# Softmax over heads beside an expert stream: expert sums and weighted values held in one PSUM bank, a third adding transfer for every two blocks, and a longer lead of experts

## The chip, the cores and the metric

The kernel runs on one core of a Trainium2 chip. A core has five engines that work beside each other and wait for each other by semaphores: TensorE (matrix products, PE in the profile, its weight loads PEld), VectorE (DVE), ScalarE (ACT), GpSimd (POOL) and SyncE (SP), which here only issues transfers. Transfers from all issuers run on 16 DMA engines. The metric is the device time of one execution in microseconds; smaller is better.

## The reference

The kernel computes a stack of eight residual layers on x of shape (2, 1024, 128). Only the last two matter here. The seventh is attention whose softmax runs over the 16 heads (axis 1 of batch, head, query, key), not over the keys. The sixth and the eighth are sums over eight gated experts.

```python
def _L1_attn_b_ref(x, w_qkv, b_qkv, w_proj, b_proj):
    qkv = (x @ w_qkv + b_qkv).reshape(b, n, 3, N_HEADS, HEAD_DIM)      # 16 heads of 8
    q, k, v = jnp.transpose(qkv, (2, 0, 3, 1, 4))
    dp = jnp.einsum('bhqd,bhkd->bhqk', q, k) * SCALE
    attn = jax.nn.softmax(dp, axis=1)                                   # over heads
    w_avg = jnp.einsum('bhqk,bhkd->bhqd', attn, v)
    return jnp.transpose(w_avg, (0, 2, 1, 3)).reshape(b, n, dim) @ w_proj + b_proj

def _L1_ffn_ref(x, Wg, Wu, Wd):                                         # 8 experts, 128 -> 512 -> 128
    return sum(jax.nn.silu(x @ Wg[e]) * (x @ Wu[e]) @ Wd[e] for e in range(8))

x = x + _L1_ffn_ref(_layernorm(x), ...)
x = x + _L1_attn_b_ref(_layernorm(x), ...)
x = x + _L1_ffn_ref(_layernorm(x), ...)
```

Because the softmax is over heads, a block of 128 queries and 128 keys needs nothing of any other block: for each of its 128x128 positions it takes the maximum over 16 heads, 16 exponentials, their sum and its inverse.

## The kernel before

All activations stay in x_res, 16 tiles of 128 tokens by 128 channels; all of the work below is float32. `first_layer` does the first six layers, up to the experts of chunks 0 and 1. Then `experts_ffn(g, w, [2])` does the experts of chunk 2 of the sixth layer (512 tokens: 32 units, one per expert and quarter of its hidden width), `heads_and_experts(g, w, [6, 7], [0, 1, 2, 3, 4, 5])` does the head softmax with an expert stream beside it, and `experts_ffn(g, w, [3])` the last experts.

**The head loop.** `heads_and_experts` writes out the order of every engine's instructions by hand (`tc.manual_schedule`). It walks 128 blocks: 2 batches, 8 query tiles, 8 key tiles. In its round i it starts block i+1 and carries older ones further. The stages of a block, with lines:

- `products` (L1194): TensorE forms the scores of all 16 heads in the four-bank PSUM tile h_s, 4 matmuls of 512 columns. There is one h_s, so the next scores wait until this block's subtraction has read it.
- `maxima` (L1205) and the subtraction (L1211) on VectorE; the result goes to h_e in SBUF, 4 buffers.
- the exponentials (L1214) on ScalarE in two halves.
- `lower` (L1220): SyncE copies heads 0 to 7 to a tile of half the size; `upper` (L1224): GpSimd issues a transfer that adds heads 8 to 15 to it. Eight sums of two heads stand there.
- `denominators` (L1229): TensorE adds these eight with identity matmuls, 8 of 128 columns, into h_pd.
- `inverse` (L1234): VectorE takes the reciprocal.
- `normalize` (L1239): GpSimd multiplies h_e by it into a second tile h_a.
- `weigh` (L1245): TensorE multiplies with the values in h_vz, 16 matmuls, into h_po. After the eighth key tile ScalarE copies h_po to h_oT (L1340), and the next round projects it (L1309) and adds it to x_res (L1318).

Round i does the scores, maximum, exponentials and `lower` of block i+1, `upper` of block i, the denominators of i-1, inverse and normalising of i-2, weighing of i-3.

**The expert stream.** `ExpertStream` feeds the same units in chunks of 256 tokens. In each round `products` (L1043) takes up to two units, each with a gate and an up product of 256 columns in one bank of e_pgu (two banks), `gates` (L1050) is the Silu on ScalarE, `multiply` (L1058) the product on VectorE, and in the next round `outputs` (L1069) multiplies by Wd, four matmuls of 128 columns, and `add` (L1078) adds them to x_res. Silu and Exp lie in different activation tables, so each round holds two table loads on ScalarE.

**The shared bank.** `outputs`, the projection and `denominators` all write h_pd, for which there is one PSUM bank. So in a round TensorE's outputs wait for the inverse that reads the last denominators, and its denominators wait for the additions that read the outputs.

**Side work.** Opening a chunk (a layer norm, two transposes) and the preparation of a batch (norm, transposes, projections) are lists of steps tagged with an engine. `aside(place)` takes one such step when the round comes to that engine; where TensorE gets a step, the round takes no expert units. Ahead of the loop the steps of batch 0 run with a round of the stream behind each. Behind the loop the stream runs alone until it is empty.

**Norms.** `StagedNorm` has three stages: statistics on VectorE, a square root on ScalarE, an inverse on VectorE. `apply_on_act` forms the shift -mean/deviation with one VectorE instruction (L74) for all tiles and applies it on ScalarE (L76); `apply` does it on GpSimd (L82).

Of the kernel before, what the change touches and what calls it, by code (L numbers as in the profile page):

```python
# [19 lines left out]
P = 128  # L20
# [28 lines left out]
class StagedNorm:  # L49
# [20 lines left out]

    def apply_on_act(self, dst):

        shift = self.g.small.tile([P, self.nt], F32, name=f"{self.key}_nb", bufs=2)
        self.g.nc.vector.scalar_tensor_tensor(shift, self.mv[:, :, 0], -1.0, self.rs, ALU.mult, ALU.mult)  # L74
        for t in range(self.nt):
            self.g.nc.scalar.activation(  # L76
                dst[:, t, :], self.src[:, t, :], AF.Identity, bias=shift[:, t : t + 1], scale=self.rs[:, t : t + 1]
            )
# [746 lines left out]
def linear_steps(g, w, b, seq, bank):  # L825
# [7 lines left out]
    for src, dst in ((xb, u), (u, un)):  # L833
        ln = StagedNorm(g, src, TPB, "l")
        ln.stats(range(TPB))
        ln.root()
        yield
        ln.inverse()
        ln.apply_on_act(dst)
        yield  # L840
# [86 lines left out]
def expert_steps(g, w, chunks, work, ps, ps_o):  # L927
# [6 lines left out]
    def opening(n):  # L934
# [7 lines left out]
        ln.inverse()  # L942
# [58 lines left out]
class ExpertStream:  # L1001

    NE, FC = 8, 4

    def __init__(self, g, w, work, ps):
        self.g, self.w, self.work, self.ps = g, w, work, ps
        self.units, self.fresh, self.gated, self.ready, self.sums = [], [], [], [], []

    def tokens(self, chunk):
        return self.g.x[:, 2 * chunk : 2 * chunk + 2, :]

    def opening(self, chunk):
# [6 lines left out]
        yield "dve", ln.inverse  # L1021
        yield "pool", lambda: ln.apply(u, range(2))

        def transposes():
# [5 lines left out]
            self.units += [(chunk, e, fc, uT) for e in range(self.NE) for fc in range(self.FC)]  # L1030

        yield "pe", transposes

    def products(self):

        nc, w = self.g.nc, self.w
        for _ in range(2):
# [24 lines left out]
    def outputs(self, po):  # L1062

        nc = self.g.nc
        if self.ready:
            two, self.ready = self.ready[:2], self.ready[2:]
            for t in range(2):
                for k, (_, e, fc, h) in enumerate(two):
                    nc.tensor.matmul(  # L1069
                        po[:, t, :], h[:, bass.ts(t, P)], self.w["Wd"][:, e, fc, :], start=(k == 0), stop=(k == 1)  # L1070
                    )
            self.sums.append((two[0][0], po))

    def add(self):

        for chunk, po in self.sums:
            xt = self.tokens(chunk)
            self.g.nc.vector.tensor_add(xt, xt, po[:, 0:2, :])  # L1078
        self.sums = []
# [12 lines left out]
def heads_and_experts(g, w, first, second):  # L1092
# [4 lines left out]
    with ExitStack() as es:  # L1097
# [10 lines left out]

        keep = one.tile([P, K], F32, name="h_keep")
# [12 lines left out]
        ex = ExpertStream(g, w, ework, ps_e)  # L1122
        qzs, kTs, vs = {}, {}, {}

        def preparation(b):

            xb = g.x[:, b * TPB : (b + 1) * TPB, :]
            ln = StagedNorm(g, xb, TPB, "h")
            u = seq.tile([P, TPB, D], F32, name="h_u", bufs=1)
            uT = seq.tile([P, L], F32, name="h_uT", bufs=1)  # L1130
            qzs[b] = seq.tile([P, K, L], F32, name="h_qz")
            kTs[b] = seq.tile([P, L], F32, name="h_kT")
            vs[b] = seq.tile([P, TPB, D], F32, name="h_v", bufs=1)
            for t in range(0, TPB, 2):
                yield "dve", lambda t=t: ln.stats((t, t + 1))
            yield "act", ln.root
            yield "dve", ln.inverse
            for t in range(0, TPB, 2):
                yield "pool", lambda t=t: ln.apply(u, (t, t + 1))


            def bias(t):
                nc.gpsimd.tensor_add(
                    xb[:, t : t + 4, :], xb[:, t : t + 4, :], w["b_proj2"].unsqueeze(1).to_broadcast([P, 4, D])
                )

            def transposes(n):
                pt = ps_e.tile([P, 4, P], F32, name="e_pgu")
                for t in range(4):
# [421 lines left out]
```

## Time and profile before

| | us |
|---|---|
| median of the runs shown | 2253.45 |
| these runs | 2245.86, 2253.45, 2253.84 |
| the profiled execution, own time | 2250.19 |
| its span, first to last instruction | 2248.2 |
| mean granted TensorE clock | 0.945 |

Stages by the profile, in microseconds from the start of the span: up to 1076 the first six layers, to 1165 the experts of chunk 2, to 1228 the preparation of batch 0, from 1227.8 (first scores) to 2122.6 (scores of the last block) the head loop, from 2158.2 the last experts. Busy time in four of these stretches:

| stretch | PE | DVE | ACT | POOL | share of the DMA engines |
|---|---|---|---|---|---|
| 1075 to 1165 | 87.33 of 90 | 23.90 | 23.45 | 1.73 | 0.00 |
| 1165 to 1250 | 66.42 of 85 | 42.90 | 35.28 | 17.19 | 0.10 |
| 1600 to 1760 | 155.18 of 160 | 144.80 | 119.14 | 124.63 | 0.59 |
| 2158 to 2248 | 84.98 of 90 | 22.68 | 21.12 | 0.00 | 0.01 |

A row of the groups view gives line, engine, operation, tiles and shapes, the number of instructions, their busy time, the mean of one in nanoseconds, and then the idle time of the engine just ahead of them with what ended it. A float32 matmul appears as two PE rows (two passes), so 16 rows of L1229 are 8 matmuls. A row of the view in order of time begins with start and duration; x32 behind it says that so many instructions are merged in it. In the transfer view the last number is the median time from the issue of a transfer to its landing.

### The profile page before, as it was taken

Reading aid. Unit: us, or ns where it says so; the run is one execution under the profiler, and the core shown is the slowest. Engines: PE = TensorE matmul, PEld = TensorE weight load, DVE = VectorE, ACT = ScalarE, POOL = GpSimd, SP = SyncE. Lnnn points to the kernel's source line nnn. Section 1 sums busy time; section 2 is a strip of 40 time slices with the busy share of each in tenths; the row PEclk is TensorE's granted clock in tenths of the full one; section 3 lists DMA queues with packets and bytes.
Section 4 is the critical chain, followed back from the end, with each engine's and each line's share of the span. In section 5 each row is a group of like instructions: output and inputs, shape, how many; then the busy total and the mean of one; then the engine's idle time right before and its main releaser. Section 6 shows DMA issues by size and latency. Waiting matters only on the chain. (4 is left out here: it accounts for less than half of the span.)

```text
span 2248.2 us, 36361 instructions
## 1 busy us (share of the span) xinstructions
PE 1967.7 (88%) x14832; PEld 1160.9 (52%) x14832; DVE 1685.6 (75%) x2030; ACT 1215.2 (54%) x1551; POOL 892.7 (40%) x464
## 2 busy tenths in 40 slices
PE   7669888889958758996998898988999999999999
PEld 4323243333334323344445676756777777777753
DVE  5866767898684699874234898988998989998822
ACT  1026512276624667744324675746777777777722
POOL 0013400073401000000001777887777777777710
PEclk9789979989988879998999999999999999999999
DMA  4000000296631386510000555555565555555500
GB/s 89 1 1 1 1 1 1 71 224 155 164 98 49 95 195 163 138 37 1 1 0 5 154 152 151 151 151 151 142 158 147 155 145 148 153 149 151 150 15 5
DMA packets 73799, 220.16 MB, mean 98 GB/s; under 512 B 9184, under 2 KB 19872, under 8 KB 73504
## 3 DMA queue, kind: packets, MB, share of 16 engines
q1 hardware_dynamic: 54736, 149.40, 22.6%
q0 software_dynamic: 18432, 67.12, 15.8%
q8 instruction: 116, 1.90, 0.4%
q10 hardware_dynamic: 464, 1.33, 0.3%
q14 instruction: 51, 0.42, 0.1%
HBM read 78.35 MB, written 5.24 MB: 37 GB/s over the span
## 5 line engine op out<-in xcount | busy, mean ns | idle before, releaser
L1239 POOL TENSOR_TENSOR h_a<-h_e,h_r 128x2048 f32<-128x2048 f32 x128 | 582.9, 4554 | 135.3 <-PE h_po L1245 90.8
L1205 DVE TENSOR_REDUCE h_m<-h_s 128x128 f32<-128x2048 f32 x128 | 293.2, 2291 | 71.1 <-PE h_s L1194 71.0
L1229 PE MATMUL h_pd<-h_e,ident 128*128 128x128 f32 x2048 | 264.4, 283 | 47.1 <-DMA h_e<-h_e 35.3
L1211 DVE TENSOR_TENSOR h_e<-h_s,h_m 128x2048 f32<-128x2048 f32 x128 | 292.4, 2284 | 2.5 <-DVE h_m L1205 0.6
L1214 ACT ACTIVATE h_e<-h_e 128x1024 f32<-128x1024 f32 x256 | 256.5, 1049 | 66.9 <-DVE h_e L1211 62.8
L1229 PEld LDWEIGHTS h_pd<-h_e,ident 128*128 128x128 f32 x2048 | 242.2, 194 | 89.7 <-DVE x_res L1078 46.7
L1050 ACT ACT_TABLE_LOAD x110 | 141.1, 1283 | 172.1 <-PE e_pgu L1043 171.8
L377 POOL TENSOR_SCALAR_AFFINE_SELECT a_pT<-a_pT 128x256 f32<-128x256 f32 x120 | 128.5, 1092 | 204.4 <-ACT a_pT L374 201.6
L279 DVE TENSOR_REDUCE a_nm<-a_s 128x2 f32<-128x1024 f32 (+7 forms) x144 | 168.0, 1217 | 41.2 <-PE a_s L270 27.3
L963 DVE TENSOR_TENSOR e_h<-e_sg,e_pu 128x512 f32<-128x512 f32 x128 | 86.6, 685 | 144.4 <-PE e_pu L956 132.1
L958 ACT ACTIVATE e_sg<-e_pg 128x512 f32<-128x512 f32 x128 | 76.4, 597 | 184.0 <-PE e_pg L955 163.9
L1069 PEld LDWEIGHTS h_pd<-Wd,e_h 128*128 128x128 f32 x1024 | 125.0, 191 | 95.0 <-DVE e_h L1058 78.8
L374 ACT ACTIVATE a_pT<-a_st 128x1024 f32<-128x1024 f32 (+3 forms) x176 | 129.9, 791 | 66.2 <-PE a_st L360 63.6
L1194 PE MATMUL h_s<-h_qz,h_kT 32*128 32x512 f32 x1024 | 148.1, 648 | 16.0 <-DVE h_e L1211 10.8
L792 DVE TENSOR_TENSOR_SCAN s_h<-s_a,s_h 128x1024 f32<-128x1024 f32 x64 | 148.7, 2324 | 17.9 <-ACT s_a L760 14.1
L1224 POOL DMA_DIRECT2D h_e<-h_e x128 | 114.6, 895 | 113.0 <-DMA h_e<-h_e 51.6
L1043 PE MATMUL e_pgu<-e_uT,Wg 128*128 128x256 f32 x512 | 155.0, 385 | 2.6 <-ACT h_qz L1158 2.1
L261 PE MATMUL a_s<-a_latT,a_qT 32*128 32x512 f32 (+3 forms) x768 | 119.8, 599 | 41.8 <-DVE a_nm L279 39.9
L1069 PE MATMUL h_pd<-Wd,e_h 128*128 128x128 f32 x1024 | 149.7, 288 | 6.5 <-DVE e_h L1058 4.7
L956 PE MATMUL e_pu<-e_uT,Wu 128*128 128x512 f32 x256 | 135.5, 612 | 20.4 <-DVE e_h L963 20.4
L1043 PE MATMUL e_pgu<-e_uT,Wu 128*128 128x256 f32 x512 | 152.8, 380 | 0.0
L1214 ACT ACT_TABLE_LOAD x111 | 142.4, 1283 | 13.3 <-issue 6.5
(283 smaller groups left out, 3231.4 us busy)
## 6 DMA issues: line engine op xcount, KB each, us to landing
h_e<-h_e SPq DMA_DIRECT2D x128, 512.0 KB, 4.1
h_e<-h_e POOLq DMA_DIRECT2D x128, 512.0 KB, 4.6
s_a<-s_steps SPq DMA_DIRECT2D x64, 512.0 KB, 5.0
s_h<-s_steps SPq DMA_DIRECT2D x64, 512.0 KB, 6.6
s_steps<-s_gate SPq DMA_DIRECT2D x8, 256.0 KB, 2.1
Wg<-in_Wg_dram SPq DMA_DIRECT2D x8, 256.0 KB, 6.0
Wu<-in_Wu_dram SPq DMA_DIRECT2D x8, 256.0 KB, 5.9
Wd<-in_Wd_dram SPq DMA_DIRECT2D x8, 256.0 KB, 6.1
```

The lines of the kernel that those rows point to most:

```text
L279: nc.vector.tensor_reduce(nm[:, half, i, h : h + together], s[:, :, :n], AX.X, ALU.max, negate=True)
L792: nc.vector.tensor_tensor_scan(h, a, h, 0.0, ALU.mult, ALU.add)
L956: nc.tensor.matmul(pu, w["Wu"][:, e, f], opened[n], start=True, stop=True)
L1043: nc.tensor.matmul(pgu[:, k, :], w[name][:, e, f], uT, start=True, stop=True)
L1050: nc.scalar.activation(sg, pgu[:, 0, :], AF.Silu)
L1069: nc.tensor.matmul(po[:, t, :], h[:, bass.ts(t, P)], self.w["Wd"][:, e, fc, :], start=(k == 0), stop=(k == 1))
L1194: nc.tensor.matmul(s[:, j, :].rearrange("p (k q) -> p k q", k=K), kTs[b][quad, bass.ts(kb, P)], qzs[b][quad, :, bass.ts(qb, P)], start=Tru ...
L1205: nc.vector.tensor_reduce(m, heads.rearrange("p h q -> p q h"), AX.X, ALU.max)
L1211: nc.vector.tensor_sub(e, heads, m.unsqueeze(1).to_broadcast([P, H, P]))
L1214: nc.scalar.activation(eh, eh, AF.Exp, scale=scale)
L1229: nc.tensor.matmul(pd, g.ident, e2[:, k, :], start=(k == 0), stop=(k == 7))
L1239: nc.gpsimd.tensor_mul(a, e, r.unsqueeze(1).to_broadcast([P, H, P]))
```

## The change

Part by part, in the order in which the stages run:

- `experts_ffn(g, w, [2])` goes; the stream's first list becomes chunks 4 to 7, that is, the two half chunks of chunk 2 come into the stream. Ahead of the head loop the stream now runs until at most 76 units are left.
- `preparation` is done in halves of a batch (512 tokens), the query tiles split with it.
- All layer norms of this stage are applied on ScalarE (`apply_on_act`), and the shift is made by `inverse_and_shift` with one VectorE instruction per tile that has one tensor and two per-partition scalars in it. This also replaces the form with two tensors in the other users of `apply_on_act`.
- One PSUM bank, `held`, takes three sums over a longer time: `sums` (256 columns, the output of a whole chunk of the stream), `po` (the weighted values) and `proj` (the projection). ScalarE zeroes a part once it is read out, and all matmuls add. `outputs` becomes one matmul of 256 columns per unit with Wd as the weights; it runs in every second round, on up to four units. The chunk's sum is copied, turned back by two transposes (`turn`) and added to x_res once per chunk.
- h_e2 becomes a tile for a pair of blocks. In even rounds GpSimd issues a third adding transfer, `fours`: for both blocks of the pair it adds the last four sums of two heads to the first four. In odd rounds `denominators` adds four sums of four heads for both blocks, 4 matmuls of 256 columns. The inverse stays one per block.
- `normalize` works in place in h_e, which has 7 buffers now. Every later stage is further behind: denominators of blocks i-3 and i-2 in odd round i, inverse and normalising of i-4, weighing of i-5, projection two rounds after the copy.
- In a round `products` of the stream now stands before `outputs`, and a round with a TensorE side step or a `turn` still takes one unit.
- Some weights move to the pool of the first layers.

```diff
+    def inverse_and_shift(self):
+        self.inverse()
+        self.shift = self.g.small.tile([P, self.nt], F32, name=f"{self.key}_nb", bufs=2)
+        for t in range(self.nt):
+            self.g.nc.vector.tensor_scalar(
+                self.shift[:, t : t + 1], self.mv[:, t, 0:1], self.rs[:, t : t + 1], -1.0, ALU.mult, ALU.mult
+            )
...
-    def outputs(self, po):
+    def outputs(self):
...
+        units, self.ready = self.ready, []
+        for chunk, e, fc, h in units:
+            last = e == self.NE - 1 and fc == self.FC - 1
+            nc.tensor.matmul(
+                self.sums, self.w["Wd"][:, e, fc, :], h, start=False, stop=last, skip_group_check=True
+            )
+            if last:
+                oT = self.work.tile([P, 2 * P], F32, name="e_oT", bufs=1)
+                nc.scalar.copy(oT, self.sums)
+                nc.scalar.copy(self.sums, self.zero.to_broadcast([P, 2 * P]))
+                self.summed.append((chunk, oT))
+    def turn(self):
+        nc = self.g.nc
+        if self.done:
+            chunk, oT = self.done.pop(0)
+            pt = self.ps.tile([P, 4, P], F32, name="e_pgu")
+            for t in range(2):
+                nc.tensor.transpose(pt[:, t, :], oT[:, bass.ts(t, P)], self.g.ident)
+            self.turned = chunk, pt
+            return True
+        self.done, self.summed = self.summed, []
+        return False
...
+        held = ps_o.tile([P, 4 * P], F32, name="h_po")
+        sums, po, proj = held[:, 0 : 2 * P], held[:, 2 * P : 3 * P], held[:, 3 * P :]
...
-            e = work.tile([P, H, P], F32, name="h_e", bufs=4)
+            e = work.tile([P, H, P], F32, name="h_e", bufs=7)
...
+        def fours(pair):
+            nc.gpsimd.dma_start(out=pair[:, :, 0:4, :], in_=pair[:, :, 4:8, :], accum_op=ALU.add)
+        def denominators(pair):
+            pd = ps_d.tile([P, 2, P], F32, name="h_pd")
+            for k in range(4):
+                nc.tensor.matmul(pd, g.ident, pair[:, :, k, :], start=(k == 0), stop=(k == 3))
             return pd
...
         def normalize(e, r):
-            a = work.tile([P, H, P], F32, name="h_a")
-            nc.gpsimd.tensor_mul(a, e, r.unsqueeze(1).to_broadcast([P, H, P]))
-            return a
+            nc.gpsimd.tensor_mul(e, e, r.unsqueeze(1).to_broadcast([P, H, P]))
...
+        def alone():
+            for place in ("dve", "act", "pool", "pe"):
+                aside(place)
+            ex.outputs()
+            ex.turn()
+            ex.add()
+            ex.products()
+            ex.gates()
+            ex.multiply()
...
+            while len(ex.units) + 32 * ex.unopened > 76:
+                alone()
...
+            for i in range(-1, n + 7):
+                now, resting, oT = resting, oT, None
                 if i + 1 < n:
                     heads = products(*blocks[i + 1])
+                even = i % 2 == 0
+                if 0 <= i - 4 < n:
+                    r = inverse(d_[i - 4 - i % 2][:, i % 2, :])
...
+                made, ex.ready = ex.ready, []
                 ex.multiply()
+                fresh, ex.ready = ex.ready, made
+                ex.products(1 if ex.turn() or aside("pe") else 2)
+                if even:
+                    ex.outputs()
+                ex.ready += fresh
...
+                    if not even:
+                        pairs[i + 1] = work.tile([P, 2, 8, P], F32, name="h_e2")
+                    lower(pairs[i + 1 - even][:, int(even)], e_[i + 1])
                 aside("dve")
+                if 0 <= i - 4 < n:
+                    normalize(e_[i - 4], r)
+                if even and 0 <= i - 2 < n:
+                    fours(pairs[i - 2])
                 if 0 <= i < n:
+                    upper(pairs[i - i % 2][:, i % 2], e_[i])
                 aside("pool")
+                if 0 <= i - 5 < n:
+                    b, qb, kb = blocks[i - 5]
+                    weigh(kb, e_.pop(i - 5))
                     if kb == TPB - 1:
...
+                        nc.scalar.copy(held[:, 2 * P :], zero.to_broadcast([P, 2 * P]))
...
+                if not even and 0 <= i - 3 < n:
+                    d_[i - 3] = denominators(pairs.pop(i - 3))
+            while ex.busy() or side or current:
+                alone()
...
-    experts_ffn(g, w, [2])
-    heads_and_experts(g, w, [6, 7], [0, 1, 2, 3, 4, 5])
+    heads_and_experts(g, w, [4, 5, 6, 7], [0, 1, 2, 3, 4, 5])
     experts_ffn(g, w, [3])
```

## The prediction

> **What bounds the kernel now.** I read the page's busy list first, then the stretch views, then one round of the head loop in order of time, then the transfers and the chain that ended last.
>
> ```profile
> span 2248.2 us, 36361 instructions
> ...
> PE 1967.7 (88%) x14832; PEld 1160.9 (52%) x14832; DVE 1685.6 (75%) x2030; ACT 1215.2 (54%) x1551; POOL 892.7 (40%) x464
> ...
> DVE  5866767898684699874234898988998989998822
> ...
> PEclk9789979989988879998999999999999999999999
> ```
>
> TensorE is busiest, but these are shares of the whole span. The tile view of h_s puts the first scores at 1227.8 us and those of the last block at 2122.6 us: 894.8 us for 127 steps, **7.05 us a block**, 40% of the span. Ahead of it stand the experts of chunk 2 (1076 to 1165 us, TensorE busy 87.33 of the 90.00 us in the stretch view) and the preparation of batch 0 (1165 to 1228); behind it lie 35.6 us until the first L955 product of the last experts (2158.2 us). Nothing else is changed in substance. One round, start, duration and engine first, idle time before it in brackets:
>
> ```profile
> 1710.33 1.08 PE L1245 MATMUL h_po<-h_a,h_vz 128*32 128x128 f32 x32
> ...
> 1711.34 1.14 PE L1194 MATMUL h_s<-h_qz,h_kT 32*128 32x512 f32 x8
> 1711.59 4.52 POOL L1239 TENSOR_TENSOR h_a<-h_e,h_r 128x2048 f32<-128x2048 f32 x1 [1.38 <-PE h_po L1245]
> ...
> 1712.41 1.16 PE L1069 MATMUL h_pd<-Wd,e_h 128*128 128x128 f32 x8
> 1712.55 2.29 DVE L1205 TENSOR_REDUCE h_m<-h_s 128x128 f32<-128x2048 f32 x1 [0.55 <-PE h_s L1194]
> ...
> 1713.41 0.60 PE L1043 MATMUL e_pgu<-e_uT,Wg 128*128 128x256 f32 x2
> ...
> 1715.09 2.28 DVE L1211 TENSOR_TENSOR h_e<-h_s,h_m 128x2048 f32<-128x2048 f32 x1
> ...
> 1715.22 2.05 PE L1229 MATMUL h_pd<-h_e,ident 128*128 128x128 f32 x16
> ...
> 1716.07 0.86 POOL L1224 DMA_DIRECT2D h_e<-h_e  x1
> ...
> 1717.20 1.08 PE L1245 MATMUL h_po<-h_a,h_vz 128*32 128x128 f32 x32
> 1717.31 0.96 DVE L1234 RECIPROCAL h_r<-h_pd 128x128 f32<-128x128 f32 x1
> ...
> 1718.19 0.69 DVE L1058 TENSOR_TENSOR e_h<-e_sg,e_pgu 128x256 f32<-128x256 f32 x2
> ```
>
> The reader is to see three chains of the same length. TensorE goes L1245, L1194, L1069, L1043, L1229 with start-to-start 1.01, 1.07, 0.89, 1.92, 1.98: 6.87 us without a real gap. VectorE goes maximum 2.21, addition 0.33 (1714.76 to 1715.09), subtraction 2.22, inverse 0.88, two products 0.66, and waits 0.55 for the next scores. GpSimd works 4.52 + 0.86 and idles. So TensorE sets the round and VectorE is 0.6 us behind. The transfers of the loop (queue, packets, MB, share of 16 engines; then KB and us to landing):
>
> ```profile
> q0 software_dynamic: 18142, 66.06, 39.3%
> q1 hardware_dynamic: 19169, 66.47, 18.8%
> ...
> h_e<-h_e POOLq DMA_DIRECT2D x126, 512.0 KB, 4.6
> h_e<-h_e SPq DMA_DIRECT2D x125, 512.0 KB, 4.2
> ```
>
> Over that stretch of 890 us, 39.3% for 126 adding transfers is 2.78 us of all 16 engines each, and 18.8% for 125 plain ones 1.34 us.
>
> **What the change takes from the loop.** Denominators: two blocks now cost TensorE 4 matmuls of 256 columns, 8 passes, in place of 2x16 passes. L1043 streams 8 such passes in 1.73 us (chain of waits), so a pair costs 1.73 + 0.15 against 2x1.98: 1.04 us off a block. Expert outputs (L1069) become one 256-column matmul a unit: 0.86 against 0.89, nothing; but their VectorE addition goes (0.33 a block), and so does the shared bank in which outputs, addition, denominators and inverse waited for each other. TensorE then needs about 1.01 + 1.07 + 1.92 + 0.86 + 0.94 = 5.80, VectorE 2.21 + 2.22 + 0.88 + 0.66 = 5.97. In-place normalising frees h_a: nothing, L1239 keeps its 4.52.
>
> **What it adds.** GpSimd issues a third transfer per pair. 256 pieces of 2 KB (two runs in each of 128 partitions) stand where the row L1224 has 128 of 4 KB (144 packets each, 16 of them tiny) for 0.88 us, so its price lies between 0.88 and 1.76. [...] I take 1.2. GpSimd: 2x4.52 + 2x0.88 + 1.2 + 0.4 of gaps = 12.4 a pair, 6.2 a block. Transfers: 2x1.34 + 2x2.78 + 2.8 = 11.0 a pair, 5.5 a block. **By resources alone the block would be 6.2 us.**
>
> **The wait that is added.** The third transfer stands on GpSimd's queue behind an even block's normalising, waits for the odd block's adding transfer, and has the second addition and the next normalising queued behind it. Its landing releases the denominators, the last TensorE work of the odd round, with the next scores queued behind them; then come the inverse and the normalising that precedes the next third transfer. That is a ring, one lap a pair:
> - normalising 4.52, and 0.05 to the issue;
> - issue to landing: c;
> - landing to denominators 0.13 (below: 1730.60 + 6.07 to 1736.81 is 0.14);
> - denominators to inverse 1.93 (8 passes of L1043 are busy from 1706.54 to 1708.43, 1.89, and 0.04 as between L1229 and L1234);
> - inverse to normalising 1.15 (L1234 at 1703.35, L1239 at 1704.50).
>
> Sum 7.78 + c. Without c TensorE would reach these denominators about 10.1 us after the inverse (the next inverse 5.97 later by VectorE's row, 1.2 for it and the first product, products 1.9, weighing 1.0), while the transfer is issued 5.7 after it, so only c up to about 4.3 is hidden.
>
> ```profile
> 1730.60 6.07 DMA h_e<-h_e
> 1736.81 2.02 PE h_pd L1229 x16
> ```
>
> c is the whole question. The nearest row is the adding transfer: median 4.6, least 4.5, most 7.1 (line view of L1224); the two lines above show 6.07 and TensorE starting right behind. [...] The row is of an accumulate of the same bytes on the same queue, so the row decides. On the 4.6 I put 0.3 for the longer issue and 0.7 for the plain transfer of the next block. That one now starts later: the changed build makes the exponential's table load (1.28 us, L1214) wait for the subtraction, whereas now the load ends just before it. [...] c = 5.6: lap 13.4, **6.7 us a block**. Ends: 4.6 (6.2 a block, GpSimd decides) and 7.1 (7.44).
>
> Loop: 127 x (6.7 - 7.05) = **-44 us**.
>
> **Around the loop.** Chunk 2's work, 64 units of 256 columns, moves from their own stage into the stream. Built order: 52 units run ahead of the first scores, 232 between first and last scores, 36 behind (before: 32, 214, 10). A lone round of two units takes 3.59 now (additions at 1188.43, 1192.02, 1195.61). The first unit's output no longer waits for the second's product, 0.43 less: 3.16. 26 rounds are 82 us, 5 for the first opening, 13 for six norms with their table loads and the projections (16 rounds now exceed 16x3.59 by 5 with one norm): the loop starts at about 1176 in place of 1228, **-50** rounded. Behind the last scores: five rounds that still carry the ring at 6.4 (32), three short ones (10), ten lone rounds (32), the last sums and opening (8): 82 against 35.6, **+46**.
> Shift from one tensor: seven more VectorE instructions of about 0.1 in each of four norms of the linear attention, the later ones beside ScalarE's 0.40 a tile: **+2**. Norms applied on ScalarE instead of GpSimd (16 e_u and 16 h_u rows, 28 us): ScalarE is busy 5.2 of 6.7, hidden; uncovered, one opening is 0.8. Weights in the early pool and the zeroing copies: nothing, beside the loop.
>
> Sum: -44 - 50 + 46 + 2 = -46 on the profiled run's own 2250.2 us, the span plus 2.0: 2204. The median of the runs, 2253.45, lies 3 us higher, so **2205 us**.
>
> **Rivals.**
> - Resources decide, c near 4.6: 6.2 a block, 127 x -0.85 = -108, total -110: **2140**. For it: the median of 4.6 holds for most adding transfers of the trace. Against: a plain transfer falls into the third one's window. Chance 0.2.
> - The ring closes later than today's round: 256 pieces cost 1.76 to issue, and the whole plain transfer (1.34) goes in between: c = 4.6 + 0.9 + 1.34 + 0.3 = 7.1, lap 14.9, 7.44 a block, +50 - 2: **2298**, slower. It decides from c = 6.35, where 127 x (P - 7.05) passes +2. For it: landings of 5.9 to 6.4 all along the chain that ended last. Chance 0.19.
> - The gain is given back exactly: c about 6.2, P 7.0 to 7.1, **2250**. Chance 0.11.
> - The change doesn't do what it says: the ring holds TensorE, so the 1.04 us of saved passes come back as idle time before the denominators. This is part of my forecast; it would look the same as the first line of it.
> The forecast itself, P between 6.45 and 6.98, has 0.5.
>
> Half a per cent, 11 us, is what can be told from no change. Faster: 0.5 + 0.2 less 0.02 at the edge, 0.68; same 0.13; slower 0.19. The range leaves out the far ends of both outer cases: 2145 to 2275.
>
> **What would show it.** Right: L1229's successor is 128-column no more and has about 512 passes, TensorE idles 1 to 1.5 us before it in odd rounds, released by a transfer; the third transfer lands after 5.2 to 6.1; first scores near 1176, some 82 us behind the last ones. Wrong: GpSimd without idle time at 6.2 a block; or an issue of the third transfer near 1.8 and landings over 6.3; or VectorE waiting for scores in every round.

## The result, and the profile after

The changed kernel takes **2362.4 us** (median of 4 runs, 2353.4 to 2364.8) against 2253.6 in the same comparison: 1.047 times the time, 95% interval 1.043 to 1.052. It is slower by 4.7% where 2% faster was forecast.

First the page of the changed kernel: the span, the busy line, TensorE's granted clock in forty slices.

```profile
span 2363.1 us, 32871 instructions
...
PE 1922.2 (81%) x12992; PEld 1063.7 (45%) x12992; DVE 1662.4 (70%) x2019; ACT 1301.4 (55%) x1698; POOL 949.5 (40%) x496
...
PEclk9889978899988799989999899999999899999899
```

TensorE's busy time has only fallen from 1967.7 to 1922.2 us; in slices 21 to 37, the head loop, the clock is no longer always full (it was 9 in all of them before); the stretch view has it at 0.89, 0.95 and 0.91 in three stretches between 1300 and 2000. The row of the scores gives the loop:

```profile
L1237 PE MATMUL h_s<-h_qz,h_kT x1024: 587/692/1218, 1195.0 to 2181.4; 32*128 32x512 f32 x171
```

and the same row of the kernel before:

```profile
L1194 PE MATMUL h_s<-h_qz,h_kT x1024: 587/692/1218, 1227.8 to 2123.0; 32*128 32x512 f32 x171
```

From 1195.0 to 2181.4 there are 127 steps of **7.77 us**, where they were 7.05 (1227.8 to 2123.0) and 6.7 was forecast. By stages, in us against the profile before: the loop starts 33 earlier, lasts 91 longer, and from the last scores to the first product of the last experts it is 92 instead of 35, 57 more. Together 115, the difference of the two spans (2363.1 and 2248.2). So the loop is the matter. Its transfers (issues with KB and median time to landing; then the rows of the two adding lines, L1266 `upper` and L1269 `fours`, duration of the issue as min/median/max in ns, and their landings):

```profile
h_e<-h_e POOLq DMA_DIRECT2D x192, 512.0 KB, 6.0
h_e<-h_e SPq DMA_DIRECT2D x128, 512.0 KB, 3.9
```
```profile
L1266 POOL DMA_DIRECT2D h_e<-h_e x128: 847/1368/2035, 1205.7 to 2199.0; - x128
DMA to landing us min/median/max: 4.5/6.9/9.9
```
```profile
L1269 POOL DMA_DIRECT2D h_e<-h_e x64: 1187/1214/1530, 1217.9 to 2204.1; - x64
DMA to landing us min/median/max: 5.0/5.3/6.9
```

The third transfer lands after 5.3 us by the median (5.6 on average), and its issue costs 1.21: both as forecast. But the ordinary adding transfer, 4.6 before, now takes 6.9. The longest waits inside the loop (who waits for whom, total, times, longest):

```profile
DVE h_r L1279 <- PE h_pd L1274: 160.5, 55, 6.5
...
POOL h_e L1283 <- DVE h_r L1279: 89.8, 38, 4.3
PE h_pd L1274 <- DMA h_e<-h_e: 82.2, 33, 4.3
...
POOL h_e L1266 <- DMA h_e<-h_e: 51.0, 18, 4.3
POOL h_e L1266 <- ACT h_e L1257: 42.2, 15, 4.5
```

VectorE waits 160 us for denominators, TensorE 82 us for the third transfer, up to 4.3 at a time, and GpSimd stands with an adding transfer at the head of its queue, 51 + 42 us. The last line names ScalarE, but the exponentials are long done there, as the next view shows: what comes last is the landing of the plain transfer. In 800 us of the loop before, the first of these waits was

```profile
DVE h_r L1234 <- PE h_pd L1229: 18.6, 20, 2.9
```

Two laps of the ring of the prediction, in order of time, cut to its members and to what stands beside them on GpSimd's queue. A lap runs from the inverse of one even block to that of the next (1699.74, 1712.56, 1730.71); the inverse at 1705.95 and the normalising at 1706.99 belong to an odd block:

```profile
1699.74 0.96 DVE L1279 RECIPROCAL h_r<-h_pd 128x128 f32<-128x128 f32 x1 [0.26 <-PE h_pd L1274]
...
1700.79 4.54 POOL L1283 TENSOR_TENSOR h_e<-h_e,h_r 128x2048 f32<-128x2048 f32 x1 [0.57 <-DVE h_r L1279]
...
1705.29 1.22 POOL L1269 DMA_DIRECT2D h_e<-h_e  x1
...
1705.95 0.95 DVE L1279 RECIPROCAL h_r<-h_pd 128x128 f32<-128x128 f32 x1
...
1706.34 1.08 POOL L1266 DMA_DIRECT2D h_e<-h_e  x1
...
1706.99 5.02 POOL L1283 TENSOR_TENSOR h_e<-h_e,h_r 128x2048 f32<-128x2048 f32 x1
...
1707.40 2.00 ACT L1257 ACTIVATE h_e<-h_e 128x1024 f32<-128x1024 f32 x2
...
1710.49 1.97 PE L1274 MATMUL h_pd<-h_e,ident 128*128 128x256 f32 x8 [0.23 <-DMA h_e<-h_e]
...
1712.56 0.96 DVE L1279 RECIPROCAL h_r<-h_pd 128x128 f32<-128x128 f32 x1 [0.56 <-PE h_pd L1274]
...
1714.94 0.86 POOL L1266 DMA_DIRECT2D h_e<-h_e  x1 [2.93 <-ACT h_e L1257]
...
1715.54 4.82 POOL L1283 TENSOR_TENSOR h_e<-h_e,h_r 128x2048 f32<-128x2048 f32 x1
...
1720.69 1.22 POOL L1269 DMA_DIRECT2D h_e<-h_e  x1 [0.33 <-issue]
...
1727.09 3.51 PE L1274 MATMUL h_pd<-h_e,ident 128*128 128x256 f32 x8 [4.22 <-DMA h_e<-h_e]
...
1730.71 0.96 DVE L1279 RECIPROCAL h_r<-h_pd 128x128 f32<-128x128 f32 x1 [6.07 <-PE h_pd L1274]
```

The first lap, inverse to inverse, takes 12.82: normalising 1.05 behind the inverse, third transfer (L1269) right behind it, denominators 5.2 after the issue, 1.97 long. The second takes 18.15. The inverse is there at 1712.56, but GpSimd stands at the odd block's adding transfer (L1266) until 1714.94, 5.5 us after that block's exponentials ended (1707.40 + 2.00). It waits for the plain transfer of heads 0 to 7 of that block, which landed at 1714.39. By the trace's packet records its packets ran from 1710.57 to 1714.07, 3.5 us where an undisturbed one takes 1.45. They ran beside those of the even block's adding transfer (issued 1706.34, landed 1714.09), which had come behind the third transfer (landed 1710.35): by 1712.5 that one had started 120 of its 128 pieces, the plain one 20 of its 128. So the third transfer reaches the plain one by way of the adding transfer behind it. This is the odd block's trouble: GpSimd stands for more than 1 us ahead of 36 of the 64 adding transfers of odd blocks, and of 4 of the even ones. So the normalising begins 2.98 behind the inverse, the third transfer goes out late, TensorE idles 4.22 us, and then the same eight passes take 3.51 instead of 1.97.

Taken over all 63 laps, from the starts and ends of these instructions (mean, us):

| term of the ring | forecast | after | e10, below |
|---|---|---|---|
| inverse to normalising | 1.15 | 1.90 | 1.04 |
| normalising, up to the third issue | 4.57 | 4.89 | 4.52 |
| third issue to start of denominators | 5.73 | 6.14 | 6.00 |
| denominators, up to the next inverse | 1.93 | 2.74 | 2.21 |
| lap | 13.38 | 15.68 | 13.77 |

### The profile page after: what moved, and what is told of

The parts are those of the page before. It is cut to its first block, busy times and chain, and to the rows that moved or that the text cites. A ratio compares the mean times of both kernels' runs of the same rounds, so it can differ in the third digit from the quotient of the medians.

```text
span 2363.1 us, 32871 instructions
## 1 busy us (share of the span) xinstructions
PE 1922.2 (81%) x12992; PEld 1063.7 (45%) x12992; DVE 1662.4 (70%) x2019; ACT 1301.4 (55%) x1698; POOL 949.5 (40%) x496
## 4 chain that ended last, share of the span: by engine, by line
PE 43%; DVE 24%; DMA 13%; ACT 8%; issue 7%; POOL 4%; SPq 0%; DVEq 0%; POOLq 0%; ACTq 0%
DMA h_e<-h_e 12%; PE h_pd L1274 5%; PE e_pgu L1060 4%; DVE a_nm L287 4%; DVE s_h L800 3%; POOL h_e L1283 3%; DVE h_e L1254 3%; DVE h_m L1248 3%; PE e_pg L963 3%; PE e_pu L964 3%; PE e_po L979 3%; PE a_s L269 3%; PE a_st L359 3%; PE h_po L1085 3%; PE s_pm L623 3%
## 5 line engine op out<-in xcount | busy, mean ns | idle before, releaser
L1283 POOL TENSOR_TENSOR h_e<-h_e,h_r 128x2048 f32<-128x2048 f32 x128 | 626.8, 4897 | 97.2 <-DVE h_r L1279 97.0
L1274 PE MATMUL h_pd<-h_e,ident 128*128 128x256 f32 x512 | 166.3, 481 | 108.5 <-DMA h_e<-h_e 89.2
L1279 DVE RECIPROCAL h_r<-h_pd 128x128 f32<-128x128 f32 x128 | 121.8, 952 | 185.3 <-PE h_pd L1274 185.3
L1266 POOL DMA_DIRECT2D h_e<-h_e x128 | 159.5, 1246 | 192.1 <-DVE h_m L1248 67.7
L1060 PE MATMUL e_pgu<-e_uT,Wg 128*128 128x256 f32 x640 | 210.3, 411 | 20.7 <-DVE e_h L1075 18.0
L1075 DVE TENSOR_TENSOR e_h<-e_sg,e_pgu 128x256 f32<-128x256 f32 x320 | 116.5, 394 | 118.0 <-ACT e_sg L1067 115.7
L1067 ACT ACTIVATE e_sg<-e_pgu 128x256 f32<-128x256 f32 x320 | 111.4, 382 | 127.1 <-PE e_pgu L1060 115.1
L1274 PEld LDWEIGHTS h_pd<-h_e,ident 128*128 128x128 f32 x512 | 116.2, 238 | 142.2 <-issue 120.9
L1085 PE MATMUL h_po<-e_h,Wd 128*128 128x256 f32 x640 | 168.4, 393 | 11.2 <-DVE e_h L1075 5.6
L1060 PEld LDWEIGHTS e_pgu<-e_uT,Wg 128*128 128x128 f32 x640 | 115.1, 197 | 117.1 <-DVE e_h L1075 84.7
L1288 PE MATMUL h_po<-h_e,h_vz 128*32 128x128 f32 x4096 | 139.4, 277 | 23.7 <-ACT h_po L1406 12.3
```

Source lines behind the costliest of these rows:

```text
L1060: nc.tensor.matmul(pgu[:, k, :], w[name][:, e, f], uT, start=True, stop=True)
L1067: nc.scalar.activation(sg, pgu[:, 0, :], AF.Silu)
L1085: nc.tensor.matmul(self.sums, self.w["Wd"][:, e, fc, :], h, start=False, stop=last, skip_group_check=True)
L1266: nc.gpsimd.dma_start(out=e2, in_=e[:, 8:16, :], accum_op=ALU.add)
L1274: nc.tensor.matmul(pd, g.ident, pair[:, :, k, :], start=(k == 0), stop=(k == 3))
L1283: nc.gpsimd.tensor_mul(e, e, r.unsqueeze(1).to_broadcast([P, H, P]))
```

## The experiments

Each is the changed kernel with one edit, unless said otherwise. Ratios are to the kernel before, with the 95% interval; "a block" is the distance of the first and the last row of the scores over 127. Capitals name the accounts set against each other before a run; "the number of LOAD" says that the result lies where the account LOAD put it, which alone doesn't prove the account.

**e1, no third transfer.**

```diff
-                if even and 0 <= i - 2 < n:
-                    fours(pairs[i - 2])
...
-            for k in range(4):
+            for k in range(8):
```

> The third adding transfer is left out; the denominators of a pair come from its eight sums, 8 matmuls of 256 columns instead of 4, all else as after the change. RING (the third transfer's landing, the denominators and the normalising that precedes the next third transfer close one lap of 15.7 us a pair): without the transfer that lap is gone, TensorE needs 5.80 - 0.94 + 1.88 = 6.7 us a block, its clock stays full, the loop falls from 7.76 to 6.8 or 6.9, so -110 to -120 us: about 2245. OTHER PARTS (in-place normalising, lags, two pair buffers for the sums, table load behind the subtraction cause the long rounds): the loop stays above 7.3, the time above 2300, and GpSimd still waits for landings of the plain transfer.

2308.7 us, 1.023 (1.021 to 1.025), 7.38 a block: 54 us are won back, but the numbers are those of OTHER PARTS, by a little. No landing holds TensorE any more, and the lap of the ring is gone, but so is the gain: the 3.72 us of sixteen passes all stand in the odd round, and VectorE waits for them (64 times, 145 us). e12 takes that apart.

**e2, normalising last.** On GpSimd's queue the third transfer and the adding transfer go ahead of the normalising, so that it no longer lies in the ring.

```diff
-                if 0 <= i - 4 < n:
-                    normalize(e_[i - 4], r)
                 if even and 0 <= i - 2 < n:
                     fours(pairs[i - 2])
                 if 0 <= i < n:
                     upper(pairs[i - i % 2][:, i % 2], e_[i])
+                if 0 <= i - 4 < n:
+                    normalize(e_[i - 4], r)
```

> Only the order on GpSimd's queue: third transfer, adding transfer, then normalising (it stood first). RING: the normalising (4.7 us and its wait) no longer stands between inverse and third transfer, so the lap reaches over two pairs and doesn't bind; TensorE's wait ahead of the denominators goes below 1 us, the denominators are back at 1.97 us, the block falls to 6.4 to 6.7, the time to 2190 to 2230. GPSIMD (its own work of 2x4.7 + 2x1.25 + 1.27 = 13.2 us a pair plus waits for landings at the head of its queue sets the pair): the block stays at 7.3 or more, or rises since normalising now stands behind waits for the plain transfer: 2310 to 2400.

2367.2 us, 1.048 (1.046 to 1.051), 7.84 a block, the number of GPSIMD. Nothing is won. TensorE no longer waits for the third transfer, but for the normalised block ahead of the weighing (L1288):

```profile
PEld h_po L1288 <- POOL h_e L1283: 181.6, 89, 4.7
...
PE h_po L1288 <- POOL h_e L1283: 139.1, 75, 4.3
...
POOL h_e L1266 <- DMA h_e<-h_e: 72.9, 27, 4.8
...
POOL h_e L1266 <- ACT h_e L1257: 57.5, 18, 4.1
```

The adding transfer still stands for landings at the head of the queue, and now every normalising is behind it, 6.65 us after its inverse on average for even blocks and 8.88 for odd ones. The wait was moved, not removed: the ring alone was too narrow an account.

**e3, expert outputs into the gap.** The outputs move from the even round to just ahead of the denominators.

```diff
-                if even:
-                    ex.outputs()
...
+                if not even:
+                    ex.outputs()
                 if not even and 0 <= i - 3 < n:
                     d_[i - 3] = denominators(pairs.pop(i - 3))
```

> The expert outputs (8 passes, 1.9 us) move from the even round to the place just ahead of the denominators in the odd round, where TensorE idles up to 4.3 us. CLOCK (idling of 2.9 us and more halves the granted clock and makes the denominators 3.1 to 3.75 instead of 1.97 us, and this lengthens the lap): idle ahead of them falls below 2.4 us, they take 1.97 nearly always (mean 2.61 before), the lap loses 0.6 us and what follows from it, 64 laps: -40 to -60 us, 2300 to 2325. NO CLOCK (slow denominators only fill time in which GpSimd's queue would have been waited for): within 15 us of 2362.

2361.0 us, 1.046 (1.043 to 1.049), the number of NO CLOCK. Yet the clock is kept nearly always, the denominators take 2.05 on average; the lap is 15.73 all the same. The 1.9 us of outputs stand in the way (third issue to denominators 7.15 instead of 6.14), and give back what the clock saves. The run shows that the slow denominators come from TensorE's pause; what they cost by themselves it can't tell.

**e4, chunk 2 back in its own stage.**

```diff
-    heads_and_experts(g, w, [4, 5, 6, 7], [0, 1, 2, 3, 4, 5])
+    experts_ffn(g, w, [2])
+    heads_and_experts(g, w, [6, 7], [0, 1, 2, 3, 4, 5])
```

(with the preparation of batch 1 from the first finished query tile on, `(1, 24, preparation(1, 0))`.)

> Chunk 2 of the sixth layer goes back to its own stage ahead of the loop, as before the change; the loop is the changed one. STAGES (moving it took 33 us off ahead of the loop and put 58 behind it, since half of the moved units run alone after the last scores): the start is 30 us later, the end 45 us shorter, the loop a little shorter where the stream runs dry: -15 to -35 us, 2325 to 2345. NEUTRAL (units cost the same wherever they run): within 10 us of 2362.

2361.4 us, 1.047 (1.044 to 1.050): neutral. The loop starts at 1241.6 instead of 1195.0, and from its last scores to the last experts it is 48 instead of 92. The kernel before had 1227.8 and 35, so with the stage where it was, the other parts of the change still cost 14 us ahead of the loop and 13 behind it.

**e5, a quarter of the bytes**, and **e6, the third transfer the other way round**: two ways to keep its issue and its place, and to take away its size or its reader. In e5 the denominators lack six of the 16 heads, in e6 eight.

```diff
-            nc.gpsimd.dma_start(out=pair[:, :, 0:4, :], in_=pair[:, :, 4:8, :], accum_op=ALU.add)
+            nc.gpsimd.dma_start(out=pair[:, :, 0:1, :], in_=pair[:, :, 4:5, :], accum_op=ALU.add)   # e5
+            nc.gpsimd.dma_start(out=pair[:, :, 4:8, :], in_=pair[:, :, 0:4, :], accum_op=ALU.add)   # e6
```

> The third transfer adds one sum to one instead of four to four, so it moves a quarter of the bytes in as many pieces; order, waits, issues and matmuls stay (the denominators lack three heads' quarter of the sums, so the output is not the reference's). LOAD (three transfers of 512 KB and two plain ones within a pair delay one another; the late plain transfer holds GpSimd's queue, and the normalising and the next third transfer behind it): plain and adding transfers land as before the change (3.4 to 4.2 and 4.6), the long laps of 18 us go, the loop comes to 6.6 to 6.9 us a block, 2220 to 2260. QUEUE (the order on GpSimd's queue and its issues set the lap, whatever the bytes): 7.5 or more a block, above 2325.

> The third transfer adds the first four sums to the last four, where nobody reads the result: the same bytes, issues and order, but the denominators no longer wait for its landing (they lack half of the heads, so the output is not the reference's). RING (the wait of the denominators for this landing, with the halved clock that follows it, makes the long laps): they go, 6.5 to 6.8 us a block, 2210 to 2250. LOAD (what the transfer does to the landings of the other transfers makes them): the block stays at 7.3 or more, above 2300, GpSimd still waits for the plain transfer.

e5: 2237.0 us, 0.992 (0.990 to 0.993), 6.90 a block, lap 13.83: the number of LOAD, but not its account. The plain transfers still land after 4.3 us and the adding ones after 5.6, GpSimd still stands for more than 1 us ahead of 33 of the 64 adding transfers of odd blocks, and the normalising is 1.63 behind its inverse on average. What is shorter is the ring's own transfer: it lands after 3.4 us, the denominators begin 4.76 after its issue instead of 6.14, only one pause ahead of them reaches 2.9 us (23 in the changed kernel), and they take 2.10 on average.

e6: 2212.1 us, 0.982 (0.980 to 0.983), **6.68 a block**. In e6 all bytes are moved, and more densely than in the changed kernel; the adding transfers land after 7.0, and normalising is later than ever (3.58 us behind its inverse). It does not matter, because the denominators no longer wait for the third transfer: TensorE idles 0.02 us ahead of them on average, 1.72 in the changed kernel. So the load alone doesn't make the long laps: they need the denominators' wait that closes the ring. e6 also shows what the loop takes without that wait, by the stretch view (us, then busy time of the engines, clock, share of the DMA engines):

```profile
1500.00:1760.00 260.00, 228.18 (x2166) 153.46 (x2165) 237.54 (x220) 218.25 (x266) 234.20 (x100) 0.99 0.84 197
...
sum 700.00, PE 616.75 PEld 417.25 DVE 636.75 ACT 576.59 POOL 633.23; mean PE 205.58 PEld 139.09 DVE 212.25 ACT 192.20 POOL 211.08
```

VectorE with 637 and GpSimd with 633 of 700 are busiest, each with 6.1 us a block. So without the denominators' wait this order of work gives 6.68, not 6.2; what makes the 0.6 between 6.1 and 6.68 no run took apart.

**e7, the table load early.** A one-column copy on ScalarE takes over the waits for the readers of the old buffer.

```diff
-        def exponentials(heads, m):
-
-            e = work.tile([P, H, P], F32, name="h_e", bufs=7)
+        def exponentials(heads, m, e):
...
+                    e = work.tile([P, H, P], F32, name="h_e", bufs=7)
+                    nc.scalar.copy(e[:, 0, 0:1], zero)
                     m = maxima(heads)
```

> A one-column ScalarE copy into the next h_e takes over the waits for the old readers of that buffer, so that the exponential's table load no longer waits for the subtraction, as before the change; nothing else. LATE TABLE (1.28 us of table load in the chain subtraction, exponential, plain transfer, adding transfer makes the adding transfer stand waiting at the head of GpSimd's queue): exponentials and plain transfers come 1.2 us earlier, GpSimd's waits for landings shrink, the block falls by 0.2 to 0.5, 2300 to 2335. NO PART: within 12 us of 2362.

2341.6 us, 1.039 (1.037 to 1.041), 7.64 a block: 21 us, between the two accounts (NO PART allowed 12, LATE TABLE asked for 27 or more). The exponentials begin 0.03 us behind the subtraction by the median; it was 1.36 in the changed kernel, and 0.41 in the kernel before. So the change made them 0.95 later, not the whole 1.28 of the load. The inverse-to-normalising term stays at 1.94. The late table load is a part of the matter, not its cause.

**e8, the plain transfer on ScalarE**: e7, and

```diff
-            nc.sync.dma_start(out=e2, in_=e[:, 0:8, :])
+            nc.scalar.copy(e2, e[:, 0:8, :])
```

> As e7, and the plain transfer of heads 0 to 7 becomes a ScalarE copy of 1024 columns (about 1.0 us); the two adding transfers and the third one stay. LOAD: the DMA engines carry 8.3 instead of 11.0 us a pair and the adding transfer no longer waits for a landing; ScalarE has 5.24 + 1.0 = 6.3 a block, below VectorE's round; 6.5 to 6.9 a block, 2215 to 2260. RING (third transfer's own landing and the normalising ahead of it): only what the shorter landing of the third transfer gives, 7.3 or more, above 2300.

2246.2 us, 0.996 (0.994 to 0.998), 6.92 a block, the number of LOAD. Without a plain landing to wait for, the normalising follows its inverse by 1.04 in all 63 laps, TensorE never idles more than 1.75 ahead of the denominators, and these take 2.02 on average. The third transfer itself is hardly sooner (6.00 to the denominators). ScalarE is now at 665 of 700.

**e9, e8 with the order of e2.**

> e8 with e2's order on GpSimd's queue: third transfer, adding transfer, normalising last. In e2 that order failed, with the adding transfer standing at the head of the queue for a landing; here there is no plain transfer. RING (in e8 the lap of 13.86 us is normalising, third transfer's landing, denominators, inverse): the normalising leaves the lap, the block goes from 6.92 to 6.6, where ScalarE at 6.3 and its side work is next: 127 x -0.3, about 2205 to 2225. SCALAR (95% busy in e8, it sets 6.9 already): within 12 us of 2246.

2239.2 us, 0.993 (0.990 to 0.996), 6.85 a block. The ring is open (TensorE pauses ahead of no denominators, they take 2.00), and the block hardly moves: with ScalarE busy 670 of 700 us this is the number of SCALAR. That ScalarE sets it is not shown: e10 has 50 us less on ScalarE, with the ring closed, and the same block.

**e10, the copy for odd blocks only.**

```diff
-                    lower(pairs[i + 1 - even][:, int(even)], e_[i + 1])
+                    if even:
+                        nc.scalar.copy(pairs[i][:, 1], e_[i + 1][:, 0:8, :])
+                    else:
+                        lower(pairs[i + 1][:, 0], e_[i + 1])
```

(on top of e7; in the even round it is the odd block's turn.)

> e7, and ScalarE copies heads 0 to 7 of the odd blocks only; the even blocks keep the plain transfer. ODD LANDING (the plain transfer of the odd block, issued while the third transfer and the even block's adding transfer move, is the one that holds GpSimd's queue; ScalarE is spared 0.5 a block against e8): waits of 1 us and more between inverse and normalising go, denominators at 1.97, 6.6 to 6.9 a block, 2210 to 2245. BOTH (the plain transfers' bytes and landings of both blocks count): in the middle between e7 and e8, 7.2 to 7.4, 2285 to 2310.

2236.6 us, 0.992 (0.989 to 0.995), 6.86 a block. Taking away 64 of the 128 plain transfers, the odd blocks', does all that e8 did, and in the ring the normalising is never later than 1.05 behind its inverse. With the 36 long waits ahead of odd blocks' adding transfers above, it is that landing which held GpSimd's queue; a copy for the even blocks only was not run. The waits in the loop:

```profile
POOL h_e L1282 <- DVE h_r L1278: 98.5, 76, 4.1
...
DVE h_r L1278 <- PE h_pd L1273: 36.7, 46, 3.0
...
PE h_pd L1273 <- DMA h_e<-h_e: 18.6, 25, 2.0
```

Against the changed kernel, over about as many blocks, VectorE's wait for denominators has gone from 160 us to 37, TensorE's for the transfer from 82 to 19, and GpSimd's long waits are for the inverse and no longer for landings.

**e11, the same copy in the kernel before** (the two lines of e8's edit), with nothing of the change.

> The kernel before, with its plain transfer replaced by the ScalarE copy of e8. TensorE sets its round at 6.87 and GpSimd idles, so a sooner landing frees nothing: within 12 us of the kernel before (2254). If instead the copy alone brings e8 its gain: 2240 or less.

2238.5 us, 0.994 (0.990 to 0.997), 6.95 a block: the copy brings 16 us there too. That is below the 2240 set for the second account, but it is not e8's gain, which was 95 us over e7. The wait view shows where: TensorE's pauses for adding transfers ahead of its denominators are 14.5 us between 1250 and 2060, 32.5 without the copy. Set beside each other over the same 700 us of loop, e10 (the change, mended) and e11:

```profile
sum 700.00, PE 604.91 PEld 407.73 DVE 618.10 ACT 620.32 POOL 613.28; mean PE 201.64 PEld 135.91 DVE 206.03 ACT 206.77 POOL 204.43
```
```profile
sum 700.00, PE 668.66 PEld 513.80 DVE 631.41 ACT 597.94 POOL 552.90; mean PE 222.89 PEld 171.27 DVE 210.47 ACT 199.31 POOL 184.30
```

TensorE has done 605 us of work in 700 in e10 and 669 in e11, and the block is only 0.09 shorter. All engines are at 605 to 620 of 700 in e10. The two times lie within each other's intervals: with the copy in both, these runs show no gain from the change.

**e12, denominators of each block again**: e1 without the pairing, 8 matmuls of 128 columns in every round.

```diff
-            pd = ps_d.tile([P, 2, P], F32, name="h_pd")
-            for k in range(4):
-                nc.tensor.matmul(pd, g.ident, pair[:, :, k, :], start=(k == 0), stop=(k == 3))
+            pd = ps_d.tile([P, P], F32, name="h_pd")
+            for k in range(8):
+                nc.tensor.matmul(pd, g.ident, pair[:, k, :], start=(k == 0), stop=(k == 7))
...
-                if not even and 0 <= i - 3 < n:
-                    d_[i - 3] = denominators(pairs.pop(i - 3))
+                if 0 <= i - 3 < n:
+                    d_[i - 3] = denominators(pairs[i - 3 - (i + 1) % 2][:, (i + 1) % 2])
```

> e1 without its pairing: no third transfer, and the denominators of one block in every round from its eight sums, 8 matmuls of 128 columns as before the change; held bank, in-place normalising, lags, order and stages stay changed. PAIRING (in e1 the 3.72 us of both blocks stand in the odd round, behind a VectorE chain that makes the even round 6.3 anyway): 6.9 to 7.05 a block, about 2250 to 2275. OTHER PARTS (held bank, lags, in-place normalising cost by themselves): 7.3 or more, as e1, 2300 and above.

2284.7 us, 1.014 (1.010 to 1.018), 7.18 a block: between the two accounts, and not back at 7.05. So third transfer and pairing together cost 78 us of the 109, and the rest of the change (lags, queue order, stages) about 30: 17 in the loop (127 x 0.13), the rest around it.

## Why the prediction was wrong

**What held.** The ring is there: TensorE stands idle ahead of the denominators in 42 of 63 laps, and without that wait (e6) the time falls by 150 us. The third transfer's price was right (c = 5.6 forecast, 5.3 to landing by the median, 5.6 on average), its issue costs 1.21 against 1.2. That is in part luck: no run shows the 0.7 that c had for the plain transfer. With no plain transfer at all (e8) the median is still 5.1, so 0.5 over the row of 4.6 is the third transfer's own and the plain ones add some 0.3 (5.07 to 5.34). The lap with GpSimd's queue free is 13.77 in e10 against 13.38. The rival with a later third transfer (c = 7.1) had the right sign for the wrong reason: the longest landing was 6.9. And none of the prediction's signs of being wrong came up: it had none for GpSimd's queue.

**What failed: the step "inverse to normalising 1.15".** It was read where GpSimd idled, and taken as a delay of two engines. In the changed kernel GpSimd often stands at the odd block's adding transfer, and the normalising is behind it in the queue; 1.15 became 1.90 on average, 1.0 to 1.1 in 34 laps and 1.8 to 4.0 in the other 29. The prediction did see the plain transfer falling into the third one's time, but charged it to c alone (0.7); it left out the even block's adding transfer, which follows the third one and meets the plain one, and it did not ask who waits for the plain transfer. It is the odd block's adding transfer, on the queue that the ring runs through. e10 shows it: with the odd blocks' plain transfers away the term is 1.04 in every lap, and the time 105 us shorter than that of e7.

**What followed from it: "denominators to inverse 1.93".** When the third transfer is that late, TensorE pauses 2.9 us and more, the trace's clock records show 0.5 granted, and 1.97 becomes 3.1 to 3.75. The mean went to 2.74. Pauses of 1 to 1.5 us, as forecast, cost nothing in this trace (all sets behind at most 1.83 us took 1.96 to 2.15); the sum counted passes at full clock throughout, and had no term for a longer pause. The trace before could have warned of it: its loop has four stretches at half clock, one of them at a pause of 1.65 us ahead of the denominators, which then took 3.31 (at 1362.3). Both terms together are 1.56 of the 2.30 us by which the lap was too short; the landing and the issue up to the denominators are 0.41, the normalising 0.32. e5 shows the ring at work from the other side: with 1.63 still at the first term, but the landing shorter, the pauses are short and the loop is at 6.90. How much of the lap the halved clock makes by itself stays open: the denominators' excess over 1.97 adds up to 0.64 x 63 = 40 us, which is at most its direct share.

**The floor of 6.2 was too low.** e6, with no wait at the denominators, gives 6.68. GpSimd was summed with 4.52 a normalising, but behind the issues it takes 5.37 by the median in e6. VectorE's inverses are 6.0 us apart in the fastest quarter of e6's rounds, as its sum of 5.97 had it, but 6.4 in the median; what delays the others is not shown. So even without the denominators' wait the change had 7.05 - 6.68 = 0.37 a block to win, 47 us, and 24 of it go around the loop; mended as in e10 it wins 0.19.

**Around the loop.** -50 + 46 was forecast; it was -33 + 57. A lone round of two units takes 3.36 where 3.16 was put (ScalarE's first Silu of the rounds ahead of the loop: 1177.48, 1180.83, 1184.19), and from the last scores to the copy of the last weighted values it is 48 instead of 42. Moving the stage was near nothing as the sum had it (e4), but the -4 in total became +24, and e4 puts it on the other parts of the change, 14 ahead of the loop and 13 behind it. The shift from one tensor: the last of the linear attention's norms begins at 1055.6 against 1051.4, 4 us where 2 was put (one such instruction takes 0.21 us, not 0.1). Norms on ScalarE and in-place normalising: of GpSimd's waits in the loop one of 3.9 us names a norm's ScalarE row; no run took either part away by itself.

## What to carry to other kernels

When a step is put on an in-order queue, follow not only the step's own wait but also what the waits of the steps already there become: here the new transfer delayed another one, whose waiting instruction stood ahead of a member of the ring. A term of a ring read in a trace where the engine was idle can be its lower end (1.15 there, 1.90 here); the same term must be asked for with the queue full, and matmul times with the pause that the ring itself makes (1.97 us, or up to 3.75 here). And before work is taken off the busiest engine, look how far behind the next one is: VectorE was 0.6 us a block behind TensorE, and where TensorE's work fell from 669 to 605 us in 700 (e11 to e10), the block fell by 0.09.

## What the runs showed of the hardware

- **TensorE's clock.** In the changed kernel, of the 64 sets of denominators all 23 behind a pause of 2.9 us or more took 3.14 to 3.75 us, all 37 behind at most 1.83 us took 1.96 to 2.15, and the four between took both. The trace's clock records show 0.5 granted in 31 stretches between 1195 and 2215 us, 17 of 3.41 us, 13 of 6.83 and one of 10.24, and each of the 23 sets falls into one of them in whole or in part. These runs show no length of pause that divides the two: of the four between, pauses of 2.28 and 2.49 us were followed by 1.97 us, those of 2.26 and 2.28 by 3.00 and 2.51; in e4 a pause of 3.45 us, in e7 one of 3.03, left the clock full, and in the kernel before one of 1.65 us was followed by 3.31.
- **GpSimd's multiplications and issues.** The multiplication of 128x2048 takes 4.52 by the median in the kernel before; in the changed kernel one behind two issues took 5.02 (at 1706.99), and in e6 the longest is 5.99. The issue of an ordinary adding transfer takes 1.37 by the median and 2.04 at most in the changed kernel, where the kernel before had 0.88 by the median.
- **A plain transfer beside an adding one.** The plain transfer of 512 KB lands after 3.0 us in e12, 3.4 in e1 and 3.9 in the changed kernel (medians), 8.5 there at its latest. In the lap shown its packets took 3.5 us beside an adding transfer, 1.45 undisturbed.
